# A cross-attention kernel over eight batches: one fp32 result unit instead of two in the first batch, the copies of q and k on another queue, nine warming products, and a new order of the first batch

## The chip, the cores and the metric

The kernel runs on one core of a Trainium2 chip. Time is device microseconds of that core for one launch, the median of several runs. The engines of the core work side by side, each through its own list of instructions in order: TensorE (PE, matrix products), VectorE (DVE), ScalarE (ACT), GpSimd (POOL) and SyncE (SP, which here only issues transfers, DMAs). ACT and POOL can issue transfers too. An instruction waits on semaphores for what it needs, and everything behind it on the same engine waits with it.

## The reference

For each of eight batches, with 512 channels and 1024 positions, in fp32:

```python
q = jnp.einsum('bcn,dc->bnd', x1, Wq) + bq
k = jnp.einsum('bcn,dc->bdn', x2, Wk) + bk[:, None]
v = jnp.einsum('bcn,dc->bdn', x2, Wv) + bv[:, None]
attn = jax.nn.softmax(jnp.einsum('bnd,bdm->bnm', q, k), axis=2)
return jnp.einsum('bcm,bnm->bcn', v, attn) + x1
```

`x1` is the input, `x2` the context; q and k have 64 channels, v has 512.

## The kernel before

Nothing is looped on the chip: the program is written out, batch after batch, from three lists of words, `FIRST` (batch zero), `MIDDLE` (batches one to six) and `LAST` (batch seven), lines 30 to 79. `follow` (line 541) turns each word into a call of the method with that name. A word such as `R.4.2` has its indices behind the points; a `+` ahead of it means that the step belongs to the next batch, a `-` to the one before. The order of the words is the order of the instructions on every engine. So in all but the last batch a list also holds the beginning of the following batch: its q, k, first scores and first splits.

The kernel reaches fp32 accuracy with fast products (type fp32r). An operand is split into a high part h (the value times 1 - 2^-13, rounded to fp32r by ACT), a low part l (the rest, from DVE) and a sum d (also DVE). Three fp32r products with these parts replace one plain fp32 product. The steps, with their words:

- Loads, all on SP's queue: `ldx1` and `ldx2` (x1 and x2, in halves), `lwq` (weights of q and k), `lsd` (the bias of v). `begin` (line 522) issues the first pieces of x2 on ACT's queue and the v weights on SP's, and then the warming products: PE multiplies a small tile of zeros (4 + 3 + 3 products, line 530) while the first data are on their way.
- q and k: `Q` and `K` project (PE, line 204), `qe` and `ke` take the result out with the bias (ACT, two instructions, line 211). Each half of the result lies on 64 partitions; `qd` and `kc` copy it to the other 64 (`repeat`, line 216: two DMAs on SP's queue). `qr` and `kr` round (ACT), `ql` and `kl` take the rest (DVE, lines 237 and 254).
- v: x2 is cut in four chunks k, split by `xh` (ACT), `xl`, `xd` (DVE). For each of eight tiles j of 128 positions, `VY` has four products, from a bank of PSUM (PE's accumulator memory) that `sy` filled with the bias (ACT), and `VX` has eight. `cy` (ACT) and `jn` (DVE) join them. `vh`, `vl`, `vd` split two tiles of v at once. In batch zero the tiles 0, 1 and 2 are made with plain fp32 products (`VF`, line 374, taken out by `jf`), since the weights' own splits (`wh`, `wl`, `wd`, `w4`) aren't ready yet.
- Scores: `S.h.i` is one tile of 128 keys against half h of the queries (two products), `Sc` copies it out (ACT). `F` takes the maximum over key tiles (DVE, four instructions), `T` over partitions (POOL, a reduction), for one quarter of the queries.
- A unit u is 128 queries, two to a quarter. `L` subtracts the maximum (DVE), `E` is the exponential (ACT), `H`, `l` and `d` split the result (ACT, DVE, DVE). `R.u.m` has the three split products of key tile m (PE, line 433), eight m to a unit. `RF.u.m` is one plain fp32 product on the unsplit data (line 458), so a unit with `RF` needs no `H`, `l`, `d`. Batch zero has two such units, 0 and 1.
- The softmax's sum of a quarter: `es` (ACT copy), `a1` (POOL issues an adding DMA), `a2`, `a3` (DVE), `tot` (POOL, a reduction), `few` (two small DMAs on SP), `rec` (DVE), `r2` (ACT).
- Results: `of` (ACT) scales an fp32 unit; a split unit has `oy` (ACT) and `o` (DVE). `oa` adds x1 by a DMA from POOL, `st` stores on SP's queue.

Buffers are shared by tags (line 119): two for `x`, two PSUM banks for q, k and scores, three each for the X and the Y products. In batch zero the odd score tiles use Y banks.

Of the kernel before, what the change touches and what calls it, by code (L numbers as in the profile page):

```python
# [23 lines left out]
T = 4096.0  # L24
# [3 lines left out]


FIRST = """  # L30
VF.0.0 VF.0.1 VF.1.0 wh.0 wl.0 wd.0 w4.0 VF.1.1 wh.1 VF.0.2 wl.1 VF.0.3 w4.1 ldx2.0 xh.1 xl.1 xd.1 VF.1.2
VF.1.3 wd.1 VF.2.0 VF.2.1 VF.2.2 VF.2.3 lwq ldx2.1 lsd K xh.2 xh.3 ldx1.0 bv ke xl.2 xl.3 ldx1.1 jf.0 jf.2
xd.3 sy.3 sy.4 sy.5 jf.1 Q kc VY.3 qe kr cy.3 vh.0 qd kl VX.3 jn.3 vh.1 qr +ldx1.0 VX.5 VX.4 xd.2 VY.4 VY.5
cy.4 cy.5 vl.1 ql S.0.0 S.0.1 S.0.2 S.0.3 Sc.0.0 Sc.0.1 vd.1 S.0.4 Sc.0.2 Sc.0.3 Sc.0.4 jn.4 S.0.5 Sc.0.5
S.0.6 Sc.0.6 vl.0 vd.0 S.0.7 Sc.0.7 F.0 T.0 S.1.1 VX.6 sy.6 VY.6 cy.6 jn.6 jn.5 vh.2 S.1.0 Sc.1.0 Sc.1.1 L.0
E.0 +ldx1.1 +Q +qe S.1.2 Sc.1.2 S.1.3 Sc.1.3 VX.7 S.1.4 Sc.1.4 RF.0.0 RF.0.1 S.1.6 F.1 S.1.7 S.1.5 RF.0.2
RF.0.3 RF.0.4 L.1 E.1 es.0 RF.0.5 +ldx2.1 Sc.1.5 Sc.1.6 Sc.1.7 vl.2 vd.2 T.1 L.2 L.3 E.3 F.2 RF.1.0 H.3 l.3
d.3 RF.1.1 RF.1.2 +ldx2.0 +K a1.0 a2.0 a3.0 E.2 H.2 es.1 l.2 a1.1 sy.7 VY.7 +qd +qr +ql RF.1.3 RF.1.4 RF.1.5
d.2 cy.7 jn.7 RF.0.6 RF.1.6 RF.0.7 RF.1.7 +ke +kc R.2.0 vh.3 T.2 L.4 L.5 E.4 E.5 H.4 H.5 F.3 tot.0 few.0 rec.0
r2.0 of.0 of.1 oa.0 oa.1 st.0 l.4 R.2.1 R.2.2 R.2.3 R.2.4 R.2.5 R.3.0 R.3.1 es.2 a1.2 a2.1 a3.1 R.3.2 R.3.3  # L40
d.4 vl.3 R.3.4 +kr +kl +S.0.0 +S.0.1 +Sc.0.0 +Sc.0.1 R.3.5 +S.0.2 +Sc.0.2 +S.0.3 +Sc.0.3 vd.3 R.2.6 R.3.6
R.2.7 R.3.7 +S.0.5 T.3 L.6 L.7 E.6 E.7 H.6 l.5 d.5 R.4.0 R.4.1 a2.2 tot.1 few.1 rec.1 r2.1 a3.2 tot.2 few.2
es.3 a1.3 l.6 st.1 oy.2 o.2 oa.2 st.2 H.7 d.6 +S.0.4 +Sc.0.4 +Sc.0.5 l.7 oy.3 o.3 oa.3 st.3 R.4.2 R.4.3 R.4.4
R.4.5 R.4.6 R.4.7 +S.0.7 d.7 +S.0.6 +Sc.0.6 +Sc.0.7 +F.0 +xh.0 +xl.0 +xd.0 a2.3 rec.2 r2.2 oy.4 +T.0 +L.0 +L.1
o.4 oa.4 st.4 R.5.0 R.5.1 R.5.2 R.5.3 R.5.4 R.5.5 R.5.6 R.5.7 oy.5 o.5 oa.5 st.5 a3.3 +E.1 +F.1 +xh.2 +xl.2
R.6.0 R.6.1 R.6.2 R.6.3 R.6.4 R.6.5 R.6.6 R.6.7 oy.6 o.6 R.7.0 R.7.1 R.7.2 R.7.3 +sy.0 +xh.1 +xl.1 +xd.1 +E.0
+es.0 +sy.1 +S.1.0 +S.1.1 +xd.2 +xh.3 +Sc.1.0 +xl.3 +Sc.1.1 tot.3 few.3 rec.3 R.7.4 R.7.5 R.7.6 R.7.7 oy.7 o.7
"""
MIDDLE = """
VY.0 cy.0 VX.0 +ldx1.0 a1.0 sy.2 jn.0 T.1 L.2 L.3 sy.3 VX.1 VY.1 cy.1 jn.1 H.1 l.1 H.0 l.0 d.0 vh.0 vl.0 vd.0  # L50
# [32 lines left out]
def kernel(  # L83
# [12 lines left out]
    nc = tc.nc  # L96
# [5 lines left out]
    H = 512  # L102
# [26 lines left out]
    def bank(tag, name):  # L129
        return psum.tile([P, H], F32, tag=tag, name=name, bufs=BUFS[tag])  # L130

    class Batch:
# [82 lines left out]

        def repeat(self, t):
            for h, r, o in ((0, lo, hi), (1, hi, lo)):
                nc.sync.dma_start(t[o, ts(h, H)], t[r, ts(h, H)])

        def Q(self):  # L220
            if self.first:
# [300 lines left out]
    def begin():  # L522
        for c in range(CT):
            states[0].hx(c)
            states[0].hw(c)
        nc.scalar.dma_start(bqk_sb, bqk)
        nc.vector.memset(warm, 0.0)
        nc.vector.memset(spark, 0.0)

        for i, times in enumerate((4, 3, 3)):  # L530
            ps = bank("Y", f"ps_warm{i}")
            for k in range(times):
                nc.tensor.matmul(
                    ps, warm, warm.unsqueeze(1).to_broadcast([P, 4, P]), start=(k == 0), stop=(k == times - 1)
                )
        nc.scalar.activation(spark, spark, AF.Exp)
# [10 lines left out]
    with tc.manual_schedule():  # L547
        begin()
        follow(FIRST, 0)
        for b in range(1, B - 1):  # L550
            follow(MIDDLE, b)
        follow(LAST, B - 1)
# [31 lines left out]
```

## Time and profile before

| | |
|---|---|
| median of 3 runs | 662.05 us (661.49 to 662.64) |
| the profiled execution's own time | 662.4 us |
| its span | 660.6 us |
| PE busy | 653.9 us |
| DVE busy | 617.3 us |
| ACT busy | 450.8 us |
| POOL busy | 199.1 us |

The span is what the profiler recorded of one execution; the run's time holds what lies around it too. In rows of the timeline the columns are the start (us from the span's start), the duration, the engine, the line of the kernel, the operation, what is written and read, the size, the count, and in square brackets how long the engine had been idle and for whom it waited. Instructions of an engine are pipelined, so a row can begin a little before the one ahead of it has ended. Matrix products show 0.39 us each while they start 0.23 us apart; their starts are to be used.

### The profile page before, as it was taken

To read this page: it belongs to the slowest core of one execution; us is meant where nothing else is said; L and a number is where in the kernel's file an instruction comes from. 1 tells how busy PE (TensorE), PEld (TensorE's weight loads), DVE (VectorE), ACT (ScalarE), POOL (GpSimd) and SP (SyncE) were. 2 spreads that over 40 slices of the span, in tenths; PEclk is the share of its full clock that TensorE was granted. 3 is DMA by queue.
4 is the path that set the end of the run, shared out by engine and by line. 5 is a ranking of instruction groups with operands and counts; after the bars stand their busy time and mean duration, and the time that the engine had idled before them with its cause. 6 is when DMAs were issued, how large, how long until landed. Compare 5 with 4: busy or idle time off the path is not lost.

```text
span 660.6 us, 8048 instructions
## 1 busy us (share of the span) xinstructions
PE 653.9 (99%) x2798; PEld 491.8 (74%) x2798; DVE 617.3 (93%) x689; ACT 450.8 (68%) x668; POOL 199.1 (30%) x162
## 2 busy tenths in 40 slices
PE   9999999999999999999999999999999999999997
PEld 3664888677886688866888668886688776887786
DVE  4699999999999999999999999999999999989994
ACT  5677757765687676876758757677675975759541
POOL 0022441423314333033420335212352214412451
PEclk9999999999999999999999999999999999999999
DMA  8634457464655646465564745737467274652274
GB/s 301 208 139 86 79 121 213 82 197 92 126 175 106 180 99 145 141 162 128 116 151 116 216 101 112 172 84 223 81 127 175 82 206 96 127 114 48 62 144 130
DMA packets 41464, 90.21 MB, mean 137 GB/s; under 512 B 13136, under 2 KB 13904, under 8 KB 37712
## 3 DMA queue, kind: packets, MB, share of 16 engines
q0 software_dynamic: 13536, 33.04, 30.0%
q1 hardware_dynamic: 27168, 56.14, 25.4%
q10 hardware_dynamic: 720, 0.53, 0.2%
q8 instruction: 22, 0.36, 0.2%
q14 instruction: 18, 0.15, 0.1%
HBM read 51.91 MB, written 16.78 MB: 104 GB/s over the span
## 4 chain that ended last, share of the span: by engine, by line
PE 77%; DVE 13%; ACT 4%; DMA 3%; issue 2%; POOL 0%; SPq 0%; DVEq 0%; POOLq 0%; ACTq 0%
PE ps_oX L433 27%; PE ps_oY L433 14%; PE ps_vX L393 13%; PE ps_s L261 7%; PE ps_vY L393 7%; PE ps_k L204 3%; PE ps_q L204 3%; DVE e L289 3%; DVE el L300 2%; PE ps_v L373 2%; DVE vd L425 1%; DVE ed L305 1%; DVE vl L420 1%; DVE max L276 1%; DMA out_dram<-o 1%
## 5 line engine op out<-in xcount | busy, mean ns | idle before, releaser
L433 PE MATMUL ps_oY<-vd,ed 128*128 128x512 f32 x496 | 193.9, 393 | 0.2 <-DVE ed L305 0.2
L433 PE MATMUL ps_oX<-vh,eh 128*128 128x512 f32 x496 | 193.0, 389 | 0.0
L433 PE MATMUL ps_oX<-vl,el 128*128 128x512 f32 x496 | 193.0, 389 | 0.0
L433 PEld LDWEIGHTS ps_oY<-vd,ed 128*128 128x128 f32 x496 | 93.1, 188 | 25.1 <-issue 5.1
L513 POOL DMA_DIRECT2D o<-in_x1T_dram x62 | 56.0, 929 | 174.5 <-ACT o L510 100.4
L433 PEld LDWEIGHTS ps_oX<-vl,el 128*128 128x128 f32 x496 | 93.0, 188 | 20.3
L433 PEld LDWEIGHTS ps_oX<-vh,eh 128*128 128x128 f32 x496 | 93.1, 188 | 19.4 <-issue 0.2
L292 ACT ACTIVATE e<-e 128x1024 f32<-128x1024 f32 x64 | 68.0, 1062 | 49.8 <-DVE e L289 48.5
L266 ACT COPY e<-ps_s 128x512 f32<-128x512 f32 x128 | 70.7, 591 | 29.1 <-PE ps_s L261 28.2
L328 POOL PARTITION_ALL_REDUCE den<-es x32 | 79.3, 2477 | 21.2 <-DVE es L318 18.2
L314 POOL DMA_DIRECT2D es<-e x32 | 28.8, 901 | 188.3 <-ACT es L311 174.0
L305 DVE SCALAR_TENSOR_TENSOR ed<-el,eh 128x1024 fp32r<-128x1024 f32 x62 | 80.2, 1294 | 2.0
L300 DVE TENSOR_TENSOR el<-e,eh 128x1024 fp32r<-128x1024 f32 x62 | 79.7, 1302 | 0.0
L289 DVE TENSOR_TENSOR e<-e,top 128x1024 f32<-128x1024 f32 x64 | 75.9, 1217 | 0.0
L408 ACT COPY vy<-ps_vY 128x512 f32<-128x512 f32 x61 | 36.0, 591 | 45.3 <-PE ps_vY L393 41.7
L393 PE MATMUL ps_vX<-wh,xh 128*128 128x512 f32 x244 | 66.2, 393 | 0.0
L281 POOL PARTITION_ALL_REDUCE top<-max x32 | 45.4, 1417 | 66.7 <-DVE max L277 66.7
L393 PE MATMUL ps_vX<-wl,xl 128*128 128x512 f32 x244 | 65.3, 389 | 0.0
L393 PE MATMUL ps_vY<-wd,xd 128*128 128x512 f32 x244 | 64.3, 391 | 0.7 <-ACT ps_vY L389 0.7
L296 ACT ACTIVATE eh<-e 128x1024 fp32r<-128x1024 f32 x62 | 64.4, 1054 | 0.4
L393 PEld LDWEIGHTS ps_vX<-wh,xh 128*128 128x128 f32 x244 | 45.2, 188 | 14.3 <-DVE max L276 4.1
L393 PEld LDWEIGHTS ps_vY<-wd,xd 128*128 128x128 f32 x244 | 45.4, 188 | 12.5 <-ACT ps_vY L389 2.5
(59 smaller groups left out, 968.8 us busy)
## 6 DMA issues: line engine op xcount, KB each, us to landing
x<-in_x_dram SPq DMA_DIRECT2D x29, 1024.0 KB, 6.9
es<-e POOLq DMA_DIRECT2D x32, 512.0 KB, 4.9
out_dram<-o SPq DMA_DIRECT2D x63, 256.0 KB, 2.4
o<-in_x1T_dram POOLq DMA_DIRECT2D x62, 256.0 KB, 4.3
x<-in_x_dram SPq DMA_DIRECT2D x5, 512.0 KB, 9.8
k<-k SPq DMA_DIRECT2D x16, 128.0 KB, 2.2
q<-q SPq DMA_DIRECT2D x16, 128.0 KB, 2.3
w_raw<-in_wvT_dram SPq DMA_DIRECT2D x4, 256.0 KB, 3.8
```

The lines of the kernel that those rows point to most:

```text
L261: nc.tensor.matmul(ps, k[:, ts(i, P)], self.qa[:, ts(h, H)], start=(z == 0), stop=(z == 1))
L266: nc.scalar.copy(self.half[h][:, :, i, :], self.ps[h, i].rearrange("p (q n) -> p q n", q=2))
L281: nc.gpsimd.partition_all_reduce(self.top[Q], self.fold[Q][:, 0, :], P, ReduceOp.max)
L289: nc.vector.tensor_tensor(e, e, top, ALU.subtract)
L292: nc.scalar.activation(self.unit(u), self.unit(u), AF.Exp)
L296: nc.scalar.activation(self.e[u]["h"], self.unit(u), AF.Copy, scale=SPLIT)
L300: nc.vector.tensor_tensor(self.e[u]["l"], self.unit(u), f32(self.e[u]["h"]), ALU.subtract)
L305: nc.vector.scalar_tensor_tensor(e["d"], f32(e["l"]), -T, f32(e["h"]), ALU.mult, ALU.add)
L328: nc.gpsimd.partition_all_reduce(self.den[Q], self.es[Q][:, 0, :], P, ReduceOp.add)
L393: nc.tensor.matmul(ps, self.c[j // 2][z][:, c, ts(j % 2, P)], w[z][:, c, :], start=(start and c == 0), stop=(stop and c == CT - 1), skip_g ...
L433: nc.tensor.matmul(ps, self.e[u][z][:, m, :], self.v[m // 2][z][:, m % 2, :], start=start, stop=stop, skip_group_check=True,)
L513: nc.gpsimd.dma_start(self.o[u], x1T[self.b, ts(u, P), :], accum_op=ALU.add)
```

## The change

In batch zero, unit 1 is computed with split products instead of plain fp32 ones: its eight `RF.1.m` and `of.1` become `H.1`, `l.1`, `d.1`, eight `R.1.m`, `oy.1` and `o.1`. Unit 0 stays fp32. `repeat` issues the copies of q and k on ACT's queue in batch zero and on SP's in all others. One warming product fewer is issued. And the whole of `FIRST` is put in another order, with the same words otherwise; `MIDDLE` and `LAST` stay.

```diff
 FIRST = """
...
+wh.0 VF.0.0 VF.1.0 wl.0 VF.0.1 VF.1.1 wd.0 w4.0 wh.1 VF.1.2 VF.1.3 wl.1 w4.1 ldx2.0 lwq VF.2.0 xh.1 VF.2.1
+xl.1 VF.2.2 xd.1 VF.2.3 ldx2.1 lsd K xh.2 xh.3 bv ke xl.2 xl.3 jf.2 kc xd.2 xd.3 sy.4 sy.5 VF.0.2 VF.0.3 jf.0
+jf.1 vh.0 sy.3 ldx1.0 ldx1.1 Q qe qd +ldx1.0 wd.1 VY.3 VY.4 VY.5 cy.3 cy.5 kr vl.0 vd.0 qr VX.3 jn.3 vh.1 VX.5
+VX.4 cy.4 kl ql S.0.0 S.0.1 S.0.2 Sc.0.0 Sc.0.1 Sc.0.2 S.0.3 S.0.4 Sc.0.3 Sc.0.4 vl.1 vd.1 S.0.5 Sc.0.5 S.0.6
+Sc.0.6 jn.4 jn.5 S.0.7 Sc.0.7 F.0 S.1.0 sy.6 Sc.1.0 vh.2 vl.2 vd.2 S.1.1 Sc.1.1 +ldx1.1 +Q +qe S.1.2 Sc.1.2
+VY.6 cy.6 S.1.3 Sc.1.3 sy.7 T.0 L.0 L.1 S.1.6 E.0 F.1 S.1.5 E.1 H.1 es.0 l.1 a1.0 +ldx2.1 VX.6 jn.6 d.1 VY.7
+cy.7 S.1.7 S.1.4 Sc.1.4 Sc.1.5 Sc.1.6 Sc.1.7 VX.7 jn.7 vh.3 RF.0.0 RF.0.1 RF.0.2 T.1 L.2 L.3 E.2 E.3 H.3 es.1
+a1.1 vl.3 vd.3 RF.0.3 RF.0.4 RF.0.5 R.1.0 R.1.1 R.1.2 RF.0.6 R.1.3 a2.0 a3.0 +ldx2.0 +K R.1.4 F.2 RF.0.7 R.1.5
++qd +qr +ql R.1.6 R.1.7 H.2 l.2 d.2 R.2.0 tot.0 few.0 +ke +kc T.2 L.5 E.5 L.4 rec.0 l.3 d.3 r2.0 of.0 oy.1
+oa.0 o.1 st.0 oa.1 st.1 a2.1 F.3 R.2.1 R.2.2 R.2.3 R.2.4 R.2.5 R.3.0 R.3.1 R.3.2 R.3.3 R.3.4 R.3.5 R.2.6 R.3.6
+R.2.7 a3.1 E.4 H.4 l.4 es.2 +kr +kl a1.2 +S.0.0 +S.0.1 +Sc.0.0 d.4 +Sc.0.1 T.3 L.6 L.7 R.3.7 H.5 l.5 a2.2
...
         def repeat(self, t):
             for h, r, o in ((0, lo, hi), (1, hi, lo)):
-                nc.sync.dma_start(t[o, ts(h, H)], t[r, ts(h, H)])
+
+                (nc.scalar if self.first else nc.sync).dma_start(t[o, ts(h, H)], t[r, ts(h, H)])
...
-        for i, times in enumerate((4, 3, 3)):
+        for i, times in enumerate((3, 3, 3)):
```

A line of the new list that begins with two plus signs begins with a word of the next batch. The old list stands in the kernel above.

More of the change, by code (lines that the diff above doesn't have):

```diff
@@ L30 @@
 FIRST = """
[L31 to L45, printed above, removed]
@@ L46 @@
-R.6.0 R.6.1 R.6.2 R.6.3 R.6.4 R.6.5 R.6.6 R.6.7 oy.6 o.6 R.7.0 R.7.1 R.7.2 R.7.3 +sy.0 +xh.1 +xl.1 +xd.1 +E.0
-+es.0 +sy.1 +S.1.0 +S.1.1 +xd.2 +xh.3 +Sc.1.0 +xl.3 +Sc.1.1 tot.3 few.3 rec.3 R.7.4 R.7.5 R.7.6 R.7.7 oy.7 o.7
+wh.0 VF.0.0 VF.1.0 wl.0 VF.0.1 VF.1.1 wd.0 w4.0 wh.1 VF.1.2 VF.1.3 wl.1 w4.1 ldx2.0 lwq VF.2.0 xh.1 VF.2.1
+xl.1 VF.2.2 xd.1 VF.2.3 ldx2.1 lsd K xh.2 xh.3 bv ke xl.2 xl.3 jf.2 kc xd.2 xd.3 sy.4 sy.5 VF.0.2 VF.0.3 jf.0
+jf.1 vh.0 sy.3 ldx1.0 ldx1.1 Q qe qd +ldx1.0 wd.1 VY.3 VY.4 VY.5 cy.3 cy.5 kr vl.0 vd.0 qr VX.3 jn.3 vh.1 VX.5
@@ new lines @@
++qd +qr +ql R.1.6 R.1.7 H.2 l.2 d.2 R.2.0 tot.0 few.0 +ke +kc T.2 L.5 E.5 L.4 rec.0 l.3 d.3 r2.0 of.0 oy.1
+oa.0 o.1 st.0 oa.1 st.1 a2.1 F.3 R.2.1 R.2.2 R.2.3 R.2.4 R.2.5 R.3.0 R.3.1 R.3.2 R.3.3 R.3.4 R.3.5 R.2.6 R.3.6
+R.2.7 a3.1 E.4 H.4 l.4 es.2 +kr +kl a1.2 +S.0.0 +S.0.1 +Sc.0.0 d.4 +Sc.0.1 T.3 L.6 L.7 R.3.7 H.5 l.5 a2.2
++S.0.2 +Sc.0.2 R.4.0 R.4.1 E.6 H.6 +S.0.3 +Sc.0.3 +S.0.4 +Sc.0.4 tot.1 few.1 rec.1 r2.1 oy.2 oy.3 R.4.2 R.4.3
+R.4.4 R.4.5 R.4.6 +S.0.5 +Sc.0.5 a3.2 d.5 R.4.7 l.6 o.2 tot.2 few.2 d.6 oa.2 st.2 +S.0.6 +S.0.7 o.3 oa.3 st.3
@@ L48 @@
++xh.0 +xl.0 +Sc.0.6 +Sc.0.7 +F.0 rec.2 E.7 H.7 es.3 l.7 a1.3 +xd.0 d.7 r2.2 oy.4 o.4 oa.4 st.4 R.5.0 R.5.1
+R.5.2 R.5.3 R.5.4 R.5.5 R.5.6 R.5.7 oy.5 o.5 oa.5 st.5 +xh.1 +xl.1 +S.1.1 +xh.2 +xl.2 a2.3 R.6.0 R.6.1 R.6.2
+R.6.3 R.6.4 R.6.5 R.6.6 R.6.7 oy.6 o.6 R.7.0 R.7.1 R.7.2 R.7.3 +S.1.0 +T.0 +L.1 +E.1 +Sc.1.0 +Sc.1.1 a3.3
++sy.0 +xd.1 +L.0 +E.0 +F.1 +es.0 +xd.2 +xh.3 +sy.1 +xl.3 tot.3 few.3 rec.3 R.7.4 R.7.5 R.7.6 R.7.7 oy.7 o.7
 """
```

## The prediction

> **What bounds the kernel now.** I read the page's engine shares first, then windows cut at the start of VectorE's (DVE's) first unbroken stretch and at batch borders, then the timelines of TensorE (PE) and DVE at the borders, and last the waits.
>
> ```profile
> PE 653.9 (99%) x2798; PEld 491.8 (74%) x2798; DVE 617.3 (93%) x689; ACT 450.8 (68%) x668; POOL 199.1 (30%) x162
> ...
> 25.37:109.16 83.79, 83.79 (x339) 59.34 (x338) 80.28 (x89) 59.75 (x88) 27.00 (x21) 1.00 0.55 136
> 109.16:189.20 80.04, 78.80 (x343) 59.51 (x342) 78.30 (x88) 56.29 (x84) 23.91 (x20) 1.00 0.58 143
> 189.20:269.50 80.30, 80.30 (x354) 62.06 (x353) 78.04 (x88) 56.57 (x84) 25.59 (x20) 1.00 0.58 138
> ...
> 102.67 1.07 PE L393 MATMUL ps_vY<-wd,xd 128*128 128x512 f32 x4
> 185.29 1.07 PE L393 MATMUL ps_vY<-wd,xd 128*128 128x512 f32 x4
> 265.54 1.07 PE L393 MATMUL ps_vY<-wd,xd 128*128 128x512 f32 x4
> ...
> 109.16 0.68 DVE L411 SCALAR_TENSOR_TENSOR v<-ps_vX,vy 128x512 f32<-128x512 f32 x1
> 189.19 0.68 DVE L411 SCALAR_TENSOR_TENSOR v<-ps_vX,vy 128x512 f32<-128x512 f32 x1
> ```
>
> Window rows give PE, PEld, DVE, ACT and POOL busy time in that order. PE is never idle from 25.37 to 109.16, but DVE is busy for 80.28 of those 83.79 us too. The next four rows decide which of the two counts. The L393 rows are VY.0, the first product of batches one to three (counting from batch zero): from 185.29 to 265.54 are 80.25 us, from 102.67 to 185.29 are 82.62. The second batch loses 82.62 - 80.25 = 2.37 us. DVE's first step in it (jn.0) stands at 109.16, in the third at 189.19, which is 108.94 less a period: DVE is 0.2 us behind its later phase, PE 2.37 us ahead of its own. PE reaches the border early and pays it back waiting. **The border's date on DVE sets the time**, and PE work taken from the first batch alone buys nothing.
>
> Where it pays back is shown by the first scores of the following batch:
>
> ```profile
> 159.31 0.39 PE L261 MATMUL ps_s<-qa,kh 128*128 128x512 f32 x1
> 160.37 0.50 PE L261 MATMUL ps_s<-qa,kl 128*128 128x512 f32 x1 [0.68 <-DVE kl L254]
> ...
> 157.96 2.36 DVE L254 TENSOR_TENSOR kl<-k,kh 128x1024 fp32r<-128x1024 f32 x1
> 238.71 1.22 DVE L254 TENSOR_TENSOR kl<-k,kh 128x1024 fp32r<-128x1024 f32 x1
> ...
> 157.96 1.99 POOL L328 PARTITION_ALL_REDUCE den<-es  x1
> 238.90 2.69 POOL L328 PARTITION_ALL_REDUCE den<-es  x1
> ```
>
> The two products start 1.06 us apart instead of 0.23: 0.83 of the 2.37 us is here, the other 1.5 earlier in the batch. The step waited for (kl) took 2.36 us when it began together with a POOL reduction, 1.22 one batch later when it began 0.19 before one. So DVE's lengths depend on what POOL is doing.
>
> **The PE terms.**
>
> ```profile
> 0.98 4.45 PE ps_warm L533 x10
> 5.43 10.37 PE ps_v L373 x24
> ...
> 161.34 0.23 PE ps_oY L433
> 161.57 0.46 PE ps_oX L433 x2
> ```
>
> A warming product is 4.45/10 = 0.44 us. An fp32 product is two passes of 10.37/24 = 0.43, so 0.86; the three split products that replace it take 0.69. A unit has eight: 8 x (0.86 - 0.69) = 1.4. PE gets 1.8 us less to do.
>
> The Trainium skill ("TensorE: Matmul & The Clock Gate", section "Part 1: The HAM clock gate (the 'warmup' mystery)") says that the slow clock ends after some 3.4 us of activity, by time and not by the number of products. The trace agrees in part: the ten warming products took 0.44 us each, about twice the 0.23 of a split product with the same 512 columns. By that rule the real work that takes the tenth product's place would itself run at half speed, and some 0.2 us of the 0.44 would be given back.
>
> **The DVE terms.** They decide, so I walk the new order up to where DVE is no longer waiting.
>
> ```profile
> 13.34 2.00 ACT L356 ACTIVATE xh<-x 128x1024 fp32r<-128x1024 f32 x2 [0.81 <-DMA x<-in_x_dram]
> 25.37 1.23 DVE L254 TENSOR_TENSOR kl<-k,kh 128x1024 fp32r<-128x1024 f32 x1 [5.05 <-ACT kh L250]
> ...
> L305 DVE SCALAR_TENSOR_TENSOR ed<-el,eh 128x1024 fp32r<-128x1024 f32 x6 | 7.3, 1222 | 0.1
> L498 DVE SCALAR_TENSOR_TENSOR o<-ps_oX,r,oy 128x512 f32<-128x512 f32 x4 | 2.9, 742 | 0.5 <-ACT oy L484 0.5
> L296 ACT ACTIVATE eh<-e 128x1024 fp32r<-128x1024 f32 x7 | 7.3, 1053 | 0.1
> ...
> DVE kl L254 <- ACT kh L250: 5.1, 1, 5.1
> DVE v L411 <- ACT vy L408: 1.0, 1, 1.0
> DVE o L498 <- ACT oy L484: 0.5, 1, 0.5
> ...
> DVE r L337 <- DMA few<-den: 0.5, 1, 0.5
> ```
>
> A wide DVE step (1024 columns) is 1.2 us, a narrow one 0.7 (0.6 from start to start), a wide ScalarE (ACT) step 1.05. Before, DVE stands idle 5.05 us ahead of kl and runs on from 25.37, with three more waits of 1.0, 0.5 and 0.5.
>
> After: K needs ten fp32 products ahead of it, not twelve, so it starts near 4.8 + 10 x 0.86 + 0.2 = 13.6 (before 15.7), just behind the context half that xh.2 also waits for until 13.34. xl.2 follows xh.2 at 14.4; with xl.3, jf.2, xd.2, xd.3, jf.0 and jf.1 (four wide, three narrow) DVE is at 20.9, with wd.1 at 22.1. vh.0 (ACT) waits for jf.1 and ends at 21.9, so vl.0 and vd.0 end at 24.5. sy.3 stands behind vh.0 on ACT and ends at 22.5, and VY.3 waits for it; Q's products would let it start at 22.3. Three VY (four products, 0.91) and VX.3 (eight, 1.8) end at 27.4 with the drain, and jn.3 waits for that. The unbroken stretch therefore **begins at 27.4, 2.0 us later**, with xd.2, vl.0 and vd.0 done ahead of it (-3.6) and l.1, d.1 and o.1 added behind it (1.2 + 1.2 + 0.7 = +3.1).
>
> Then two handoffs from ACT are late in the new order. S.0.0 starts at 30.8 behind VX.5 and VX.4. The eight Sc, sy.6 and Sc.1.0 start 0.48 us apart (row below) from 31.4, so vh.2 runs from 36.2 to 37.25, while DVE is through F.0 at 36.7: vl.2 waits 0.6. +Q keeps PE until 38.9, and +qe, Sc.1.2, cy.6, Sc.1.3, sy.7, E.0, E.1 and H.1 are queued behind it on ACT (1.4 + 2.0 + 3.2): H.1 ends at 45.7, while DVE is through F.1 at 44.4. l.1, which is new, waits 1.3. Behind that every input lies ready ahead of DVE: es.0's sum lands before a2.0, H.2 ends at 56.6 and l.2 starts at 58.9, oy.1 ends at 65.4 and o.1 starts at 66.1.
>
> ```profile
> 116.73 0.96 ACT e L266 x2
> ...
> 55.89 2.17 DVE L300 TENSOR_TENSOR el<-e,eh 128x1024 fp32r<-128x1024 f32 x1
> 58.09 2.00 DVE L237 TENSOR_TENSOR qa<-q,qa 64x1024 fp32r<-64x1024 f32 x1
> 57.34 2.38 POOL L328 PARTITION_ALL_REDUCE den<-es  x1
> ```
>
> Sum for DVE at the border: +2.0 - 3.6 + 3.1 + 0.6 + 1.3 - (1.0 + 0.5 + 0.5) = **+1.4 us**. It takes the stretching by POOL as unchanged: the same nine reductions fall in the batch, but on other steps. The rows above show two steps stretched by 0.8 to 0.95 each; one pair more or less is +-1.7. The old wait for few may come back, +0.5. I take the middle, since no row favours an end.
>
> **ACT's terms.** H.1 adds 1.05 us, which the walk contains; oy.1 costs what of.1 did. The copies' four issues move to ACT:
>
> ```profile
> 0.72 1.85 ACTq L166 DMA_DIRECT2D x<-in_x_dram  x4
> 25.98 1.02 SPq L148 DMA_DIRECT2D x<-in_x_dram  x2
> ...
> k<-k SPq DMA_DIRECT2D x2, 128.0 KB, 2.2
> q<-q SPq DMA_DIRECT2D x2, 128.0 KB, 3.3
> q<-q SPq DMA_DIRECT2D x2, 128.0 KB, 7.0
> ```
>
> An issue costs ACT 1.85/4 = 0.46. The pair for k falls where ACT would only wait for jf.1, the pair for q ahead of cy.3, while ACT waits for VY.5 anyway (25.5): nothing. On SP, the next batch's x1, two loads of 1 MB, no longer stands behind the copies and goes at 19 instead of 25.98. The copies then share the engines with it. Their landing is bounded by 2.2 and 7.0 us (the last row: behind 2 MB on one queue). I take 3.3, the nearest row, since the copies now have a queue of their own: q's second half, issued at 24.4, lands at 27.7, qr ends at 28.8, ql at 30.1, and S.0.0 keeps 30.8. At 7.0, S.0.0 starts at 33.9.
>
> **From the border to the end.** PE stays 1.8 us or less ahead and waits more; that costs nothing by itself. At the scores of the following batch PE is 0.83 us plus its drain, about 1.0, early before. With DVE 1.4 later it is 0.4 late there. kl would start at 159.4 and end at 160.6 if POOL leaves it alone, against 160.32 before: 0.3 late. Both say +0.3 to +0.4; every later batch is the old order at 80.25. The profiled execution's span of 660.6 becomes 660.9, and with the 1.8 us around it (its own time was 662.4) 662.7; that execution lay 0.35 over the median of 662.05, so the median becomes **662.4**.
>
> **Rivals.** A difference under 0.2%, 1.3 us, can't be told from none here.
> (1) *DVE holds the border, little changes*, as summed: 662.4, own range 661.2 to 663.3. Chance 0.47. For it: DVE's 80.28 of 83.79.
> (2) *PE's gain arrives.* The two ACT waits don't appear, or swallow stretches that POOL would cause, and kl escapes the reduction: DVE +1.4 - 1.9 = -0.5, and with the 1.0 that PE has in hand -1.5, which is 660.5; with one stretched pair less -3.2, which is 658.8. Middle: about 659.7. For it: 1.8 us of PE work are really gone and 2.37 can be won back. Against it: DVE's list grew. Chance 0.20.
> (3) *Slower, POOL falls badly.* kl starts with a reduction again (2.36, not 1.22), or one pair of steps more is stretched: +0.3 + 1.1 to 1.7, about 663.8. It decides once a reduction starts at or before kl. For it: the row at 157.96; against: the one at 238.71. Chance 0.20.
> (4) *Slower, q's copy comes late beside the 2 MB.* Landing after 28.4 moves S.0.0; at 7.0 us it is 33.9 - 30.8 = +3.1 for PE and DVE alike, about 665.4. For it: the 7.0 row; against: that was one queue. Chance 0.13. The Trainium skill ("DMA: Bandwidth & Descriptors", section "Queues, rings and completion order") says that a DMA engine goes round its queues packet by packet, which would favour a landing near 3.3; no run here shows the two queues side by side with such loads.
>
> Faster is (2), 0.20; no change is (1), 0.47; slower (3) and (4), 0.33. The range holds (1) and (3) and the nearer parts of the others: 659.6 to 665.0.
>
> **What would show it.** Right: the border step jn.0 at 110.0 to 111.0, waits of DVE for vh.2 and H.1 near 37 and 45, VY.0 of the third batch within 1.3 us of 185.29, PE waiting longer in the second batch. Wrong: jn.0 below 108, S.0.0 after 31.5, or periods other than 80.25 later on.

## The result, and the profile after

The changed kernel takes 664.2 us (median of 10 runs, 663.21 to 667.67) against 662.42 for the kernel before (10 runs, 661.49 to 663.0): a ratio of 1.0034, 95% interval 1.0018 to 1.0051. It is slower by 1.2 to 3.4 us. The time lies inside the range that was forecast, 659.6 to 665.0, and 1.8 us over its middle of 662.4; that no change could be measured was held likeliest. Measured again on another chip the ratio was 1.0020 (1.0008 to 1.0033).

The page's engine line, the windows cut at DVE's unbroken stretch and at its border step jn.0 (columns as before: PE, PEld, DVE, ACT, POOL), and the timelines of PE and DVE at the borders of the changed kernel:

```profile
PE 653.2 (99%) x2805; PEld 492.3 (74%) x2805; DVE 620.0 (94%) x692; ACT 452.4 (68%) x669; POOL 201.3 (30%) x162
...
27.93:112.30 84.37, 81.43 (x336) 58.22 (x335) 80.44 (x90) 58.52 (x86) 26.71 (x21) 1.00 0.46 108
112.30:191.58 79.28, 78.82 (x343) 59.84 (x342) 77.69 (x87) 56.45 (x84) 25.58 (x20) 1.00 0.59 145
...
105.60 0.73 PE L394 MATMUL ps_vY<-wd,xd 128*128 128x512 f32 x2 [0.73 <-ACT ps_vY L390]
187.52 0.61 PE L394 MATMUL ps_vY<-wd,xd 128*128 128x512 f32 x2
267.67 0.62 PE L394 MATMUL ps_vY<-wd,xd 128*128 128x512 f32 x2
...
112.30 0.67 DVE L412 SCALAR_TENSOR_TENSOR v<-ps_vX,vy 128x512 f32<-128x512 f32 x1
```

(Lines behind the edit are one higher than before.) DVE's border step stands at 112.30, 3.14 us later than before's 109.16. PE's own first product of the second batch stands at 105.60, 2.93 later than 102.67, although PE has 1.8 us less to do: PE now shows 81.43 busy of 84.37 in the first stretch, where it was never idle. So PE's gain went into waits. In the third batch the kernel is 187.52 - 185.29 = 2.23 us late, at the end of the span 662.3 - 660.6 = 1.7.

Who waited for whom, PE over the whole run and DVE from 20 to 105 us (engine, line, releaser: total us, times, longest), and the landing times of the copies of k and q, from the DMA view of the same kernel:

```profile
PE ps_vY L394 <- ACT ps_vY L390: 1.4, 3, 0.7
PE ps_s L262 <- DVE kl L255: 1.0, 1, 1.0
PE ps_s L262 <- DVE qa L238: 0.7, 1, 0.7
...
DVE v L412 <- PE ps_vX L394: 3.3, 1, 3.3
DVE qa L238 <- ACT qa L235: 1.1, 1, 1.1
DVE el L301 <- ACT eh L297: 1.0, 1, 1.0
DVE vl L421 <- ACT vh L416: 0.5, 1, 0.5
...
k<-k ACTq DMA_DIRECT2D x2, 128.0 KB, 7.4
q<-q ACTq DMA_DIRECT2D x1, 128.0 KB, 5.5
q<-q ACTq DMA_DIRECT2D x1, 128.0 KB, 5.1
```

The waits at jn.3 (3.3), H.1 (1.0) and vh.2 (0.5) are those of the prediction's walk. The wait of ql for qr (1.1) is not: the copy of q took 5.1 to 5.5 us, not the 3.3 that was taken, and k's 7.4.

A second profile of the same kernel, from the other chip, has an earlier border step. Its row, and the landings of q's copy there (least, median, most):

```profile
111.22 0.67 DVE L412 SCALAR_TENSOR_TENSOR v<-ps_vX,vy 128x512 f32<-128x512 f32 x1
...
DMA to landing us min/median/max: 4.2/4.4/4.6
```

The step is 2.06 us late there, not 3.14. DVE's waits are 3.4, 1.1, 0.5 and 0.4 us, and none of them is ql's. So q's copy was late against the 3.3 us in both executions, but it cost DVE 1.1 us in only one.

### The profile page after: what moved, and what is told of

The parts are those of the page before. It is cut to its first block, busy times and chain, and to the rows that moved or that the text cites. A ratio compares the mean times of both kernels' runs of the same rounds, so it can differ in the third digit from the quotient of the medians.

```text
span 662.3 us, 8063 instructions
## 1 busy us (share of the span) xinstructions
PE 653.2 (99%) x2805; PEld 492.3 (74%) x2805; DVE 620.0 (94%) x692; ACT 452.4 (68%) x669; POOL 201.3 (30%) x162
## 4 chain that ended last, share of the span: by engine, by line
PE 83%; DVE 9%; ACT 3%; DMA 2%; issue 1%; DVEq 0%; SPq 0%; ACTq 0%
PE ps_oX L434 31%; PE ps_oY L434 16%; PE ps_vX L394 13%; PE ps_s L262 8%; PE ps_vY L394 7%; PE ps_q L204 4%; PE ps_k L204 4%; DVE e L290 2%; DMA x<-in_x_dram 1%; DVE el L301 1%; DVE max L277 1%; PE ps_v L374 1%; DMA q<-q 1%; DVE v L412 1%; ACT e L293 1%
## 5 line engine op out<-in xcount | busy, mean ns | idle before, releaser
L434 PE MATMUL ps_oY<-vd,ed 128*128 128x512 f32 x504 | 197.5, 394 | 0.5 <-DVE ed L306 0.5
L434 PE MATMUL ps_oX<-vh,eh 128*128 128x512 f32 x504 | 196.3, 390 | 0.0
L434 PE MATMUL ps_oX<-vl,el 128*128 128x512 f32 x504 | 196.1, 389 | 0.0
L434 PEld LDWEIGHTS ps_oY<-vd,ed 128*128 128x128 f32 x504 | 94.6, 188 | 27.9 <-issue 7.0
L434 PEld LDWEIGHTS ps_oX<-vh,eh 128*128 128x128 f32 x504 | 94.6, 188 | 20.0 <-issue 0.7
L434 PEld LDWEIGHTS ps_oX<-vl,el 128*128 128x128 f32 x504 | 94.6, 188 | 19.8
L329 POOL PARTITION_ALL_REDUCE den<-es x32 | 81.4, 2545 | 24.3 <-DVE es L319 17.8
L306 DVE SCALAR_TENSOR_TENSOR ed<-el,eh 128x1024 fp32r<-128x1024 f32 x63 | 83.4, 1323 | 2.0
L301 DVE TENSOR_TENSOR el<-e,eh 128x1024 fp32r<-128x1024 f32 x63 | 81.7, 1312 | 1.0 <-ACT eh L297 1.0
```

Of the source, the lines that this page charges most:

```text
L301: nc.vector.tensor_tensor(self.e[u]["l"], self.unit(u), f32(self.e[u]["h"]), ALU.subtract)
L306: nc.vector.scalar_tensor_tensor(e["d"], f32(e["l"]), -T, f32(e["h"]), ALU.mult, ALU.add)
L329: nc.gpsimd.partition_all_reduce(self.den[Q], self.es[Q][:, 0, :], P, ReduceOp.add)
L434: nc.tensor.matmul(ps, self.e[u][z][:, m, :], self.v[m // 2][z][:, m % 2, :], start=start, stop=stop, skip_group_check=True,)
```

## The experiments

Two theories run through them. **D**: the date at which VectorE comes to the batch border sets the time, and PE work taken away or added in the first batch counts only as far as it moves that date. **P**: the time follows PE's work. Q, L and A are named where they are used. Ratios are to the kernel before on the same chip, with 95% intervals. The kernel before with two more DVE steps was executed five times, the others 11 or 12 times.

| kernel | median, us | ratio |
|---|---|---|
| copies on SP's queue | 662.96 | 1.0008 (0.9999 to 1.0017) |
| unit 1 in fp32 | 661.61 | 0.9993 (0.9985 to 1.0002) |
| before, DVE + 2 steps | 664.77 | 1.0035 (1.0022 to 1.0047) |
| before, PE + 2 products | 662.91 | 1.0008 (0.9999 to 1.0017) |
| order alone | 660.89 | 0.9981 (0.9972 to 0.9990) |
| order alone, again | 661.25 | 0.9980 (0.9971 to 0.9989) |
| order alone, kl early | 660.86 | 0.9978 (0.9969 to 0.9986) |
| next x1 behind the copies | 663.69 | 1.0023 (1.0015 to 1.0032) |
| before, nine warming products | 662.28 | 0.9998 (0.9990 to 1.0007) |
| before, vd3 moved | 661.80 | 0.9994 (0.9985 to 1.0003) |
| changed kernel, again | 663.46 | 1.0020 (1.0008 to 1.0033) |

### Which engine sets the time

Work was added to the kernel before, on one engine at a time. On DVE, in `d`:

```diff
+            for _ in range(2 if self.first and u in (4, 6) else 1):
                 nc.vector.scalar_tensor_tensor(e["d"], f32(e["l"]), -T, f32(e["h"]), ALU.mult, ALU.add)
```

> The kernel before, with d.4 and d.6 of batch zero computed twice (the same values are written again): VectorE has two wide steps more, 2.4 us, late in the batch. Theory D: jn.0 at 111.6 instead of 109.2, and the time longer by 1.3 to 2.4 us, 663.7 to 664.8. Rival P: no change, 662.4.

On PE, in `RF`, ahead of the product with m = 0 of unit 1:

```diff
+            for _ in range(2 if (u, m) == (1, 0) else 0):
+                nc.tensor.matmul(
+                    self.X[u], self.unit(u)[:, m, :], self.v4[m // 2][:, m % 2, :], start=True, stop=True
+                )
```

> The kernel before, with two more fp32 products in front of unit 1 of batch zero, whose result is overwritten: TensorE has 1.7 us more to do, VectorE nothing. Theory D: TensorE reaches the border 1.7 us later, still ahead of VectorE, and the time stays within 0.4 us of 662.4. Rival P: 664.1.

The border step in the timelines of the two kernels, DVE's first, then PE's:

```profile
111.17 0.68 DVE L412 SCALAR_TENSOR_TENSOR v<-ps_vX,vy 128x512 f32<-128x512 f32 x1
```

```profile
109.36 0.68 DVE L411 SCALAR_TENSOR_TENSOR v<-ps_vX,vy 128x512 f32<-128x512 f32 x1
```

2.4 us more on DVE moved the border by 2.0 and the time by 0.35%, 2.3 us. 1.7 us more on PE moved the border by 0.2 and the time by 0.08%, 0.5 us, with an interval that includes zero and reaches 1.1: short of 1.7, though 662.91 is 0.1 over what D had allowed. D holds, P is out. In its first batch the kernel before is bound by VectorE's date at the border, not by its 99% busy PE.

The profiles of all runs bear this out. Each row has DVE's border step (jn.0), PE's first product of the third batch (VY.0), the time between the two, and the end of the span, in us:

| profile | jn.0 | VY.0, third batch | between | end |
|---|---|---|---|---|
| before | 109.16 | 185.29 | 76.13 | 660.6 |
| before, DVE + 2 steps | 111.17 | 187.28 | 76.11 | 662.6 |
| before, PE + 2 products | 109.36 | 185.46 | 76.10 | 660.8 |
| before, nine warming products | 109.46 | 185.61 | 76.15 | 660.9 |
| before, vd3 moved | 108.84 | 184.93 | 76.09 | 659.7 |
| changed kernel | 112.30 | 187.52 | 75.22 | 662.3 |
| changed kernel, again | 111.22 | 186.46 | 75.24 | 661.2 |
| copies on SP's queue | 111.28 | 186.51 | 75.23 | 661.3 |
| next x1 behind the copies | 111.79 | 187.05 | 75.26 | 661.8 |
| unit 1 in fp32 | 109.74 | 184.97 | 75.23 | 659.7 |
| order alone | 109.89 | 184.94 | 75.05 | 659.7 |
| order alone, again | 108.61 | 183.60 | 74.99 | 658.3 |
| order alone, kl early | 109.06 | 184.06 | 75.00 | 658.8 |

The border's dates spread over 3.7 us, but the time between is 76.1 in the old order and 75.0 to 75.3 in the new one: the third batch begins a fixed time after DVE's border step. PE's own date doesn't do that. With two more DVE steps it began the second batch at 105.79, 3.12 us late, partly because its clock was halved for a while (last section), and still was only 1.99 late in the third batch, as DVE had been at the border (2.01).

### What each edit costs

The copies back on SP's queue, in the changed kernel:

```diff
-                (nc.scalar if self.first else nc.sync).dma_start(t[o, ts(h, H)], t[r, ts(h, H)])
+                nc.sync.dma_start(t[o, ts(h, H)], t[r, ts(h, H)])
...
-... VF.2.3 ldx2.1 lsd K xh.2 ... vh.0 sy.3 ldx1.0 ldx1.1 Q qe ...
+... VF.2.3 ldx2.1 lsd ldx1.0 ldx1.1 K xh.2 ... vh.0 sy.3 Q qe ...
```

> The changed kernel with the copies of q and k back on SyncE's queue in batch zero; the loads of x1 stand ahead of the copies on that queue, as in the kernel before. Theory D (the date at which VectorE reaches the batch border sets the time): q's copy lands 3.3 us after its issue, not 5.1, the 1.1 us that ql waited for qr goes, jn.0 moves from 112.3 to about 111.2 and the time from 664.2 to about 663.1. Rival Q (the copies' late landing is the whole loss): 662.4, as before. Rival P (the time follows TensorE's work): 664.2, no change.

Unit 1 in plain fp32, in the changed kernel:

```diff
-... E.1 H.1 es.0 l.1 a1.0 +ldx2.1 VX.6 jn.6 d.1 VY.7 ... R.1.0 R.1.1 ... oy.1 oa.0 o.1 st.0 ...
+... E.1 es.0 a1.0 +ldx2.1 VX.6 jn.6 VY.7 ... RF.1.0 RF.1.1 ... of.1 oa.0 st.0 ...
```

> The changed kernel with unit 1 in plain fp32 again: no H.1, l.1, d.1, oy.1 and o.1, eight fp32 products in place of 24. TensorE has 1.4 us more to do, VectorE 3.1 us less and no wait of 1.0 for H.1. Theory D: jn.0 near 108.2, 4 us earlier than in the changed kernel, and a time of 661.0 to 662.4. Rival Q: 664.2. Rival P: 665.6.

Both together, which leaves the new order and nine warming products:

> The changed kernel with both of its other edits undone: the copies on SyncE's queue (x1's loads ahead of them) and unit 1 in plain fp32; what is left is the new order and nine warming products. Theory D (VectorE's date at the border sets the time): jn.0 about 1 us earlier than with unit 1 alone undone (109.74), near 108.8, and 660.6 to 661.2. Rival: the two edits' costs are not additive, since one wait hides in the other: 661.6, as with unit 1 alone undone.

DVE's border steps, of the copies on SP, of unit 1 in fp32, and of the order alone (its first and its second profile):

```profile
111.28 0.68 DVE L412 SCALAR_TENSOR_TENSOR v<-ps_vX,vy 128x512 f32<-128x512 f32 x1
```

```profile
109.74 0.68 DVE L412 SCALAR_TENSOR_TENSOR v<-ps_vX,vy 128x512 f32<-128x512 f32 x1
```

```profile
109.89 0.67 DVE L412 SCALAR_TENSOR_TENSOR v<-ps_vX,vy 128x512 f32<-128x512 f32 x1
```

```profile
108.61 0.68 DVE L412 SCALAR_TENSOR_TENSOR v<-ps_vX,vy 128x512 f32<-128x512 f32 x1
```

Against the first profile of the changed kernel (112.30) the copies' return won 1.0 us at the border, as D expected, and the unit's 2.6 rather than 4; against the second (111.22) the copies' return won nothing there and the unit's 1.5. Rival Q, that the copies were the whole loss, would have left unit1_fp32 at 664.2; it came to 661.61. **The unit is the larger cost**: between the order alone (0.9981) and the same with the unit split (copies on SP, 1.0008) lie 0.27%, 1.8 us, and the intervals don't meet. The copies cost 0.12 to 0.26% (from 1.0008 to 1.0020 and 1.0034), 0.8 to 1.7 us; the interval of 1.0008 meets that of 1.0020 but not that of 1.0034, so that they cost anything is likely rather than shown.

The order alone missed its date in the first profile (109.89, expected 108.8) and met it in the second (108.61); the last section tells why dates of single executions differ so much. In time it met what was expected, and it is **faster than both kernels**: 0.2% under the kernel before, twice. Its border is not the reason: 109.89 and 108.61 lie on both sides of 109.16. By the table it wins 1.1 us between the border and the third batch, where kl takes 1.22 us and not the 2.36 of the kernel before, and then 0.1 us in each later batch (80.15 instead of 80.25, last section).

> The order alone once more, beside the changed kernel on one chip: 660.4 to 661.4, 0.15 to 0.25% under the kernel before.

> The changed kernel once more on the chip of the other two: 663.5 to 664.8, 0.2 to 0.4% over the kernel before.

Side by side on one chip they were 661.25 and 663.46 us, the first as expected and the second 0.04 below its range.

### Why the copies land late

The next batch's x1 was moved behind the copy of q, on the same queue of ACT:

```diff
-                nc.sync.dma_start(t, src)
+                (nc.scalar if self.b == 1 else nc.sync).dma_start(t, src)
...
-... Q qe qd +ldx1.0 wd.1 ... S.1.1 Sc.1.1 +ldx1.1 +Q +qe ...
+... Q qe qd +ldx1.0 +ldx1.1 wd.1 ... S.1.1 Sc.1.1 +Q +qe ...
```

> The changed kernel with the next batch's x1 (two loads of 1 MB) issued on ScalarE's queue right behind the copy of q, not on SyncE's at 17.6 us. The copies stay on ScalarE's queue. Theory L (the copies land late because the 2 MB are under way beside them): k's copy lands in 2 to 3 us instead of 7.4, q's in 2 to 3.5 instead of 5.1, ql no longer waits 1.1, jn.0 near 111.3, the time near 663.2 (ScalarE pays about 1 us for the two issues where it has waits). Rival Q (ScalarE's queue itself is slow for them): landings as in the changed kernel and 664.2.

Landings of k's copy and of q's copy in this kernel (least, median, most), and DVE's waits for them:

```profile
DMA to landing us min/median/max: 2.2/2.2/2.2
```

```profile
DMA to landing us min/median/max: 3.1/3.3/3.4
```

```profile
DVE v L412 <- ACT vy L409: 3.4, 1, 3.4
DVE el L301 <- ACT eh L297: 1.0, 1, 1.0
DVE kl L255 <- ACT kh L251: 0.9, 1, 0.9
```

On ACT's queue, with the 2 MB issued behind them and not ahead, the copies land in 2.2 and 3.3 us instead of 7.4 and 5.1 (6.8 and 4.4 in the second profile). So it is the loads, not the queue (theory L). ql no longer waits. But the two issues hold ACT up ahead of cy.3 and kr, and kl now waits 0.9 for kr. The time, 663.69, lies 0.5 over what L expected, and its ratio of 1.0023 is no better than the changed kernel's second, 1.0020: no gain in time is shown. That what the landings won was paid for with ACT's time is argued from kl's wait. Moving the copies had freed SP's queue, and what the freed queue did first was to issue 2 MB at 17.6 us, ahead of the copies (18.3 and 23.8).

### A wait filled, and nothing won

In the order alone, kr was put ahead of qe and kl ahead of jn.3, into DVE's wait of 3.3 us:

```diff
-... vh.0 sy.3 Q qe qd ... cy.3 cy.5 kr vl.0 vd.0 qr VX.3 jn.3 ... cy.4 kl ql S.0.0 ...
+... vh.0 sy.3 kr Q qe qd ... cy.3 cy.5 vl.0 vd.0 kl qr VX.3 jn.3 ... cy.4 ql S.0.0 ...
```

> The order alone (copies on SyncE's queue, unit 1 in fp32), with kr ahead of qe on ScalarE and kl ahead of jn.3 on VectorE, so that kl fills 1.2 of the 3.3 us in which VectorE stands waiting for VX.3. Theory D with waits that swallow: VectorE stands again at jn.7 for TensorE's VX.7 (2.7 us), so the 1.2 us are lost there, jn.0 stays near 109.9 and the time near 660.9. Rival: time won at any wait of VectorE counts, jn.0 near 108.7 and 659.7.

DVE's waits from 20 to 115 us in the order alone, and then with kl early:

```profile
DVE v L412 <- PE ps_vX L394: 5.9, 2, 3.3
DVE el L301 <- ACT eh L297: 0.7, 1, 0.7
DVE vl L421 <- ACT vh L416: 0.6, 1, 0.6
DVE e L290 <- POOL top L282: 0.4, 1, 0.4
```

```profile
DVE v L412 <- PE ps_vX L394: 5.0, 2, 2.7
DVE vl L421 <- ACT vh L416: 0.8, 1, 0.8
DVE el L301 <- ACT eh L297: 0.7, 1, 0.7
DVE max L277 <- ACT e L267: 0.6, 2, 0.3
DVE e L290 <- POOL top L282: 0.4, 1, 0.4
DVE qa L238 <- ACT qa L235: 0.3, 1, 0.3
DVE max L275 <- ACT e L267: 0.2, 1, 0.2
```

The wait for VX.3 became shorter by 1.0, and the waits at ql (0.3), in F.0 (0.6 and 0.2) and at vl.2 (0.2 more) became longer. The sums are 7.6 and 8.0 us, and the times 0.9980 and 0.9978. The waits swallowed it, though at ql, F.0 and vl.2 and not at jn.7, where it had been expected (2.6 before, 2.7 now). The border step came at 109.06, between the two expectations; dates of single executions differ by more than that (last section), so the time decides. By this reading only work moved past the last wait for PE, or an earlier PE, could bring the border forward in this order; that wasn't tried.

### Two that concern no edit of the order

> The kernel before with nine warming products, not ten. Theory D: the products behind begin up to 0.4 us earlier, VectorE's first steps wait for data and not for them, and the time stays within 0.4 us of 662.2. Rival P (TensorE's work): 661.8. If the slow clock ends by time and not by the count of products, the first fp32 product takes some 0.2 us longer than before.

(In the kernel before, `enumerate((3, 3, 3))`.) Nothing in the time: 0.9998. The first fp32 product took 0.74 us longer (1.87 instead of 1.13), not 0.2. What it shows of the clock stands in the last section.

> The kernel before, with the buffer of vd's fourth tile set aside first, so that it lies at another place of SBUF than its last 4.5 KB (all later buffers move up by 4 KB); no instruction changes. Theory A (the place of that buffer makes the 16 products of a batch that read it start 234 ns apart instead of 227): from the second batch on all products are 227 ns apart, a period of 80.15 us instead of 80.25, and the time 0.5 to 0.8 us shorter, near 661.6. Rival: the 7 ns come from the order of the work, and nothing changes: 662.2.

```diff
+        new([P, 2, C], "vd3", "vd_early", FR)
         nc.vector.memset(warm, 0.0)
```

It bought 0.06% by the ratio, with an interval that includes zero; the period tells more, below.

## Where the prediction was right, and where it was not

The range held 664.2, but not because the sum was right: it had been made wide enough for two rivals, and what came is a part of each. That the kernel is slower, which had been given a chance of 0.33, is shown (1.0034 and 1.0020, both intervals above 1). Two of the prediction's own signs of being wrong appeared: S.0.0 came after 31.5 (32.13, and 31.60 in the second profile), and later periods were not 80.25.

**The bound** was right: DVE's date at the border decides, shown by the two loads of work. **PE's term** of 1.8 us bought nothing, as predicted.

**The first step that failed is q's copy**: "I take 3.3, the nearest row, since the copies now have a queue of their own". It took 5.1 to 5.5, and 4.2 to 4.6 in the second profile, between the bounds of 2.2 and 7.0 that the text had given. The queue of its own did not keep it at 3.3 beside the 2 MB. The price in the first profile: ql waited 1.1 us for qr, and S.0.0 started at 32.1, not 30.8. This is rival (4) at part of its size (it was priced with 7.0 us, +3.1); in the second profile that price was not paid.

**The DVE sum** was +1.4, measured +3.14 in the first profile and +2.06 in the second. For the first the terms can be given. The stretch began at 27.93, not 27.4 (+0.5); ql's wait (+1.1); the waits for vh.2 and H.1 were 1.5 together, not 1.9 (-0.4). The term that was taken as unchanged, POOL's stretching, grew: adding up what DVE steps took over their usual length gives 6.6 us after and 5.7 before (+0.9), with ten POOL reductions ahead of the border in both (the prediction had counted nine). The new d.1 is one of those steps, and F.2's two middle steps (1.38 undisturbed) another; timeline of DVE and POOL in the changed kernel:

```profile
49.04 2.22 DVE L306 SCALAR_TENSOR_TENSOR ed<-el,eh 128x1024 fp32r<-128x1024 f32 x1
58.22 2.60 DVE L277 TENSOR_TENSOR max<-max,e 128x512 f32<-128x512 f32 x2
...
49.26 1.37 POOL L282 PARTITION_ALL_REDUCE top<-max  x1
58.16 2.09 POOL L329 PARTITION_ALL_REDUCE den<-es  x1
```

Those four are +2.1, where 1.7 were missing; the rest, -0.4, is spread over small steps and not traced further.

**The way from the border to the end** was right in kind and size. It was to turn +1.4 into +0.3 to +0.4, a gain of about 1.0. It turned +3.14 into +2.23, and +2.06 into +1.17 in the second profile: 0.9 in both. kl escaped the reduction, as had been assumed:

```profile
161.11 1.22 DVE L255 TENSOR_TENSOR kl<-k,kh 128x1024 fp32r<-128x1024 f32 x1
```

Where kl was stretched again, in the kernel before with two more DVE steps (2.36 us), nothing was gained on this way (2.01 became 1.99).

**The later period** was wrong by a little and in the change's favour: 267.67 - 187.52 = 80.15 us instead of 80.25, because the change also moved a buffer (last section), which the prediction did not consider. Over the batches that follow this gave back the 0.5 us that lie between +2.23 and +1.7.

**The copies' issues on ACT** cost nothing visible where they were put: ACT waits for jf.1 and VY.5 behind them, as said. **H.1 and the split of unit 1** were in the walk at 3.1 us of work and 1.3 of waiting; undoing them moved the border by 1.5 to 2.6 us and the time by 1.8 (order alone against copies on SP) to 2.7 us (from 1.0034 to 0.9993). Undoing the copies is worth 0.8 to 1.7 us with unit 1 split and 0.12%, 0.8 us, with unit 1 in fp32 (0.9993 to 0.9981); whether the two edits simply add can't be told from that.

## What to carry to other kernels

When two engines are both full, compare where each of them stands at a boundary with where it stands one period later: the engine that is early there is not the one to relieve. Moving a small transfer to a free queue also frees the queue that it leaves, and the large transfers behind it start earlier, beside the small one; find out what the freed queue issues first. Time won at one wait can be lost at the next: in the run with kl early 1.0 us was won at VX.3 and lost at later waits. And when a new order wins, ask where: here it was behind the border that had been in view.

## What the runs showed of the hardware

**The slow clock's end differs from run to run.** Start and length of the warming products and of the two passes of the first fp32 product, from timelines of four executions, cut where the third pass would begin: the kernel before, the same with nine warming products, the order alone in its first profile and in its second:

```profile
0.98 4.45 PE L533 MATMUL ps_warm<-warm 128*128 128x512 bf16 x10 [0.98 <-DVE spark L528]
5.22 1.13 PE L373 MATMUL ps_v<-w_raw,x 128*128 128x512 f32 x2
```

```profile
0.98 4.02 PE L533 MATMUL ps_warm<-warm 128*128 128x512 bf16 x9 [0.98 <-DVE spark L528]
4.79 1.87 PE L373 MATMUL ps_v<-w_raw,x 128*128 128x512 f32 x2
```

```profile
0.98 4.02 PE L534 MATMUL ps_warm<-warm 128*128 128x512 bf16 x9 [0.98 <-DVE spark L529]
4.79 1.56 PE L374 MATMUL ps_v<-w_raw,x 128*128 128x512 f32 x2
```

```profile
0.98 3.55 PE L534 MATMUL ps_warm<-warm 128*128 128x512 bf16 x9 [0.98 <-DVE spark L529]
4.37 1.02 PE L374 MATMUL ps_v<-w_raw,x 128*128 128x512 f32 x2
```

The two passes took 1.13, 1.87, 1.56 and 1.02 us, and nine warming products 4.02 or 3.55. In the second execution the passes began 0.43 us earlier than in the first and were still done later (4.79 + 1.87 = 6.66 against 5.22 + 1.13 = 6.35): the slow clock was simply longer there. In the last one it had ended before the ninth warming product did, by 4.5 us (0.98 + 3.55). So one warming product more or fewer decides nothing, which is what the 0.9998 says.

The Trainium skill, "TensorE: Matmul & The Clock Gate", section "Part 1: The HAM clock gate (the 'warmup' mystery)", says that the clock is raised by a stretch of time in which the engine is busy, not by a count of products. The runs agree that it isn't a count: the last two executions are one kernel with nine warming products each, and only one was at full speed before the ninth ended. A fixed time from the first product they don't show either.

It also bears on how single executions are compared. The last two are one kernel. By the end of the first fp32 product they are 4.79 + 1.56 - 4.37 - 1.02 = 0.96 us apart, at DVE's border step 109.89 - 108.61 = 1.28. Most of that difference is thus there from the start; that it was carried through is argued from the two numbers. The changed kernel's two border steps are 1.08 apart. A date of one profile is thus good to about 1 us here. The changed kernel's lateness stands above that in both profiles (3.14 and 2.06), unit 1's less clearly (2.6 and 1.5), and what the copies' return won at the border (1.0 and nothing) does not; those two rest on the ratios.

**A product's period depended on where its input lay.** The first vY product of the third and of the fourth batch, PE's timelines of the kernel before (the fourth batch; the third stands in the prediction, 265.54) and of the same with vd3 moved:

```profile
345.80 1.07 PE L393 MATMUL ps_vY<-wd,xd 128*128 128x512 f32 x4
```

```profile
265.07 1.07 PE L393 MATMUL ps_vY<-wd,xd 128*128 128x512 f32 x4
...
345.22 1.07 PE L393 MATMUL ps_vY<-wd,xd 128*128 128x512 f32 x4
```

The period is 345.80 - 265.54 = 80.26 us in the one and 345.22 - 265.07 = 80.15 in the other, as in the changed kernel (80.15). In the kernel before, the 16 products of a batch that read vd's fourth tile start 234 ns apart, where the others start 227 ns apart: 16 times 7 ns is the 0.11. That tile was the last of the program's buffers, 4 KB at the highest addresses that it used in each partition of SBUF; in the changed kernel, and with vd3 moved, result tiles lie there, and the 16 products start 227 ns apart like the others. The run changed nothing but the places of buffers, so the place is the cause. Why that one is slower stays open.

PE is busy for all of such a period (80.25 of the 80.25 us from 265.54 to 345.79), so here a few ns per product count, as they didn't in the first batch.

**PE's clock was halved once more in some executions.** A window of the kernel before with two more DVE steps; the columns are as before, and the figure behind the five engines is the granted clock:

```profile
76.00:79.45 3.45, 3.45 (x10) 2.71 (x9) 3.42 (x4) 2.25 (x5) 0.00 (x0) 0.51 0.21 61
```

The products in it start 0.43 us apart. One such stretch makes the mean granted clock of an execution 0.997 (3.45 x 0.49 / 662.6 is 0.0026), and six executions have that mean: three of the five of this kernel (664.39, 664.77 and 665.05 us; the other two took 664.2 and 665.6, so its verdict doesn't hang on it), and the three longest of the 22 of the changed kernel (667.67, 667.03 and 666.44). All other executions whose clock is on record have 0.999 or 1.0. Without its three, the changed kernel's medians would be 663.85 and 663.13 us, 1.4 and 0.6 over the kernel before. What halves the clock stays open. In the execution shown PE had just stood for 1.96 us waiting for kl, at 72.5, but no run tests whether that is the reason.
